# Layer 1's last turns as moves through DRAM, shared sends, and a fetch in pieces: a conv-attention and recurrence kernel in f32

## The chip, the core and the metric

The kernel runs on one core of a Trainium2 chip. The metric is the device time of one execution in microseconds, the median of several runs. A span is the part of it that the profiler sees from the first to the last instruction of the program.

## What is computed

The input x is [4, 128, 64, 64] in f32: 4 batches, 128 channels, 4096 positions. All arithmetic is f32. The reference, cut to what matters:

```python
# layer 0: attention over 4096 positions with 64 channels of q and k, gated, residual
x = x + conv_attn(group_norm(x))      # softmax(q.T k * scale), v and gate through sigmoids
# layer 1
t = x as tokens                       # [B, 4096, 128]
h = layernorm(t)
q = h @ W;  scores = q @ q.T          # symmetric: scores(n, a) is the transpose of scores(a, n)
t = t + softmax(scores) @ h
h2 = layernorm(t)
Wx = batchnorm(h2 @ Wf)               # statistics over all batches and positions
y_t = sigmoid(Wx_t + y_{t-1} @ V.T)   # recurrence over the positions
x = (t + y) as channels by positions
```

## The kernel before

The program goes through the batches one after the other: layer 0 of a batch (`layer0`), then its layer 1 (`layer1`), and after the last batch the recurrence for all of them.

**Blocks and steps.** The 4096 positions are eight blocks of 512 (`QB`, `NB`), numbered n. Layer 1 visits the query blocks in the order 6, 7, 5, 4, 3, 2, 1, 0, and for each n the key blocks a from n down to 0. Since the scores are symmetric, only a <= n is computed. One pair (n, a) takes two steps (i = 0, 1) of 256 keys each. A step computes scores on TensorE (L810), takes the exponential on ScalarE (L816), and appends the result e to a queue `fifo`; two steps later `direct` (L681) multiplies e by the values h into the sum o of block n.

**The other half of the scores.** For a < n, the transposed exponentials are needed for block a. `turn_tiles` (L651, L645) transposes 32x32 blocks on VectorE into one of two buffers dd, `send` (L661) moves these blocks to their places in one of three buffers tt by 16 DMAs from SBUF to SBUF (4 values of p times 4 of f), and four steps later `reversed_products` (L694) multiplies tt by the values of block n into `oacc` of block a. SP's queue issues the sends with f = 0, 1, 2; the four with f = 3 wait in `unsent` and are issued by ACT's queue, one entry per step, after the step's exponential.

**Blocks on the diagonal.** Where a == n > 1 (`upper`), only the upper triangle of 128x128 tiles is computed: scores of 512, 384, 256 and 128 columns. The tiles off the diagonal are turned and sent too (24 KB per DMA), and `own_products` (L671) adds them three steps later, after `direct` of that step. Blocks 0 and 1 compute the first half in full, and `quarter` (L590, L596) computes the last quarter of the scores and transposes the missing one on TensorE.

**End of a block.** When all parts of a block are in `oacc`, `finish` puts small functions into a queue `pending`; each step of layer 1 runs one of them. `tokens` transposes oacc on TensorE (L736), takes the denominators (L741), adds the residual t (L745) and takes the layer norm. `turn` transposes the normed tokens h2 on TensorE (L758) and copies them to th on ScalarE (L759); `result` writes t for the end. `inputs` multiplies th by the recurrence's weights (L767), takes the statistics and stores the result in wxs_d in DRAM, in the last batch in wxs. A placeholder `nothing` runs an item of a second queue, `ahead`, that holds the next batch's norm and projections; a step with nothing pending does the same.

**Moves.** In layer 0 a turn of 128x512 goes another way, `move`: VectorE transposes 32x32 blocks (L280), four DMAs write them to DRAM in their new order (L284), and one DMA fetches the whole (L294).

**wxs.** At the start of the last batch's layer 1 three DMAs of 2 MB fetch the recurrence's inputs of the first three batches (L947). They share a buffer with layer 0's projections, and wait until layer 0 has read these.

**Order.** The program text gives priorities; a planner with costs of its own then fixes the order of each engine's instructions, except in stretches that are marked as ordered by hand (the beginning and the end).[...]

Of the kernel before, what the change touches and what calls it, by code (L numbers as in the profile page):

```python
# [10 lines left out]
F32 = mybir.dt.float32  # L11
I32 = mybir.dt.int32
AF = mybir.ActivationFunctionType
ALU = mybir.AluOpType
# [4 lines left out]
P = 128  # L19
# [153 lines left out]
def fast(  # L173
# [17 lines left out]
    with ExitStack() as st:  # L191
# [368 lines left out]
        def layer1(b, h, qt):  # L560
# [7 lines left out]
            fifo: deque = deque()  # L568
            own_turned: deque = deque()

            unsent: deque = deque()
            turned: deque = deque()
            clock = 0
# [39 lines left out]

            def upper(n, a):

                return a == n > 1

# [45 lines left out]
            def own_products():  # L665

                _, n, t, o = own_turned.popleft()
                assert fifo and fifo[-1][0] == n
                t = t[:, : 4 * 6 * 32].rearrange("q (p s k) -> q p s k", p=4, s=6)
                for j, s in ((3, 3), (2, 1), (1, 0)):  # L670
                    nc.tensor.matmul(  # L671
                        o[:, : j * P], lhsT=h[:, NQ * n + j, :],
                        rhs=t[:, :, s : s + j, :].rearrange("q p k j -> q k p j"),
                        start=False, stop=False,
                    )
# [25 lines left out]
            def part(n, o):  # L701
# [7 lines left out]
                if parts[n] == NB - n - (b == B - 1 and n == 0):  # L709
                    finish(n)  # L710

            def finish(n):
                cs = bass.ts(n, QB)
                rinv = stat.tile([P, NQ], F32, tag="rinv", name="rinv")
                t = work.tile([P, 4, NQ, 32], F32, tag="t", name="t1", bufs=2)
                if b == B - 1 and n == 0:

                    one, two = (ep.tile([P, 2, QB], F32, tag="e", name="last") for _ in range(2))
                    h2, t1 = (one[:, r, :].rearrange("q (j c) -> q j c", j=NQ) for r in range(2))
                    th = two[:, 0, :]  # L720

                    def bank():
                        return ps_o.tile([P, QB], F32, tag="o", name="ml")
                else:
                    h2 = work.tile([P, NQ, C], F32, tag="h2", name="h2")
                    th = work.tile([P, QB], F32, tag="th", name="th")
                    t1 = work.tile([P, NQ, C], F32, tag="og", name="t1b")

                    def bank():
                        return ps_m.tile([P, QB], F32, tag="m", name="m1")  # L730
                nc.sync.dma_start(t, t_d[b, n])

                def tokens():
                    m = bank().rearrange("q (j c) -> q j c", j=NQ)
                    for j in range(NQ):
                        nc.tensor.transpose(m[:, j, :], oacc[:, n, bass.ts(j, P)], ident)  # L736
                    if b == B - 1 and n == 0:
                        take_banks()
                    at = (B + b) * NT + n * NQ
                    den = den_all[:, at : at + NQ]  # L740
                    nc.vector.tensor_reduce(den, m, AX.X, ALU.add)  # L741
                    nc.vector.tensor_scalar(den, den, 1.0 / C, None, ALU.mult)
                    nc.vector.reciprocal(rinv, den)
                    for j in range(NQ):
                        nc.vector.scalar_tensor_tensor(  # L745
                            t1[:, j, :].rearrange("q (p i) -> q p i", p=4),
                            m[:, j, :].rearrange("q (p i) -> q p i", p=4), rinv[:, j : j + 1],
                            t[:, :, j, :], ALU.mult, ALU.add,
                        )
                    layernorm(quarters(t1), quarters(h2))  # L750

                def result():
                    turn_out(t1.rearrange("q j (p i) -> q j p i", p=4), t2_d[b, :, cs])

                def turn():
                    m = bank()
                    for j in range(NQ):
                        nc.tensor.transpose(m[:, bass.ts(j, P)], h2[:, j, :], ident)  # L758
                    nc.scalar.copy(  # L759
                        th.rearrange("c (p j k) -> c j p k", j=NQ, p=4),  # L760
                        m.rearrange("c (j p k) -> c j p k", j=NQ, p=4),
                    )
                    result()

                def inputs():
                    m = bank()
                    nc.tensor.matmul(m, lhsT=wt["f"], rhs=th, start=True, stop=True)  # L767
                    nc.vector.bn_stats(bn_st[:, b * NB + n, :], m)
                    m = m.rearrange("p (g i s) -> p i g s", i=L // 2, s=2)
                    if b == B - 1 and n == 0:  # L770
                        last_inputs.append(m)
                    elif b == B - 1:
                        nc.vector.tensor_copy(wxs[:, :, b, bass.ts(n, GB), :], m)
                    else:
                        wx = work.tile([P, L // 2, GB, 2], F32, tag="wx", name="wx")
                        nc.vector.tensor_copy(wx, m)
                        nc.sync.dma_start(wxs_d[b, :, :, bass.ts(n, GB), :], wx)

                if b == B - 1 and n == 0:
                    pending.appendleft(tokens)  # L780
                    pending.extend([turn, inputs])
                elif b == B - 1 and n == 1:
                    pending.extend([tokens, nothing, turn, inputs])
                elif b == B - 1 and n < 4:
                    pending.extend([tokens, turn, inputs])
                else:
                    pending.extend([tokens, nothing, nothing, nothing, turn, inputs])


            for n in [NB - 2, NB - 1] + list(range(NB - 3, -1, -1)):  # L790
# [4 lines left out]
                for a in order(n):  # L795
# [4 lines left out]
                    for i in range(2):  # L800
                        ps = ps_s.tile([P, 2, QB], F32, tag="s", name="ps")
                        e = ep.tile([P, 2, QB], F32, tag="e", name="e")
                        if a == n < 2 and i == 1:
                            quarter(n, ps, e, before)
                        else:
                            width = 0
                            for half in range(2):
                                at = NQ * a + 2 * i + half
                                cols, scores = columns(n, a, i, half, ps)
                                nc.tensor.matmul(  # L810
                                    scores, lhsT=qt[:, bass.ts(at, P)],
                                    rhs=qt[:, n * QB + cols.start : n * QB + cols.stop],
                                    start=True, stop=True,
                                )
                                width += cols.stop - cols.start
                            nc.scalar.activation(  # L816
                                e.rearrange("p a b -> p (a b)")[:, :width],
                                ps.rearrange("p a b -> p (a b)")[:, :width], AF.Exp, bias=shift,
                            )
                            if turns(n, a) or upper(n, a):  # L820
                                turn_tiles(n, a, i, e, packed(d, n, a))
# [9 lines left out]
                            queries(NB - 1)  # L831
                        fifo.append((n, a, i, e, o))
                        clock += 1
                        if len(fifo) > LAG:
                            direct()
                            if a == order(n)[0] and i == 0:
                                direct()
                        if own_turned and own_turned[0][0] <= clock:
                            own_products()
                        if turned and turned[0][0] <= clock:  # L840
                            reversed_products()
                        if pending:
# [1 line left out]
                        elif ahead:  # L844
                            ahead.popleft()()
                    if turns(n, a) or upper(n, a):
                        send(n, a, d, t, nc.sync, range(3))
                        unsent.append(partial(send, n, a, d, t, nc.scalar, (3,)))
                    if upper(n, a):
                        own_turned.append((clock + 3, n, t, o))  # L850
                    elif turns(n, a):
# [83 lines left out]
        for b in range(B):  # L935
            xg, q, k, v = parts0
            h, qt = layer0(b, xg, q, k, v, need)
            need = lambda n, p: None
            if b < B - 1:
                parts0, norm, chunks, gates = prepare(b + 1, own_bank)  # L940
                ahead.extend(norm + sum(chunks, []) + gates)
            else:


                wxs = keep.tile([P, L // 2, B, G, 2], F32, tag="next", name="wxs")
                for i in range(B - 1):
                    nc.sync.dma_start(wxs[:, :, i, :, :], wxs_d[i])  # L947
            layer1(b, h, qt)
            while ahead:
                ahead.popleft()()  # L950
# [491 lines left out]
```

## Time and profile before

| What | Value |
|---|---|
| median of 3 runs | 3017.7 us (3017.13 to 3018.09) |
| the profiled execution, its time | 3015.99 us |
| its span | 3014.3 us |
| mean granted TensorE clock | 0.995 |
| layer 1, sends of full tiles on SP's queue | 1332 of 64 KB, 2.0 us to landing |
| layer 1, sends of full tiles on ACT's queue | 444 of 64 KB, 2.0 us to landing |
| fetches of wxs | 3 of 2048 KB, 13.8 us to landing |

How to read the profile: PE is TensorE's matrix multiplication, PEld its weight load, DVE VectorE, ACT ScalarE, POOL GpSimd, SP the engine that only issues DMAs. A "q" after an engine's name is its queue. A group line gives the line of the kernel, the engine, the operation, what it writes and reads, the shapes and the count; then the busy time in us and the mean in ns of one, and after a second bar the idle time of the engine just before these instructions, with what ended it. Lines in order of time begin with the start and the length in us. The chain gives the shares of the span on the path that ended last. An f32 matmul shows as two records, and matmuls overlap, so the distance between starts says more of the cost than the duration of one.

### The profile page before, as it was taken

To read this page: it belongs to the slowest core of one execution; us is meant where nothing else is said; L and a number is where in the kernel's file an instruction comes from. 1 tells how busy PE (TensorE), PEld (TensorE's weight loads), DVE (VectorE), ACT (ScalarE), POOL (GpSimd) and SP (SyncE) were. 2 spreads that over 40 slices of the span, in tenths; PEclk is the share of its full clock that TensorE was granted. 3 is DMA by queue.
4 is the path that set the end of the run, shared out by engine and by line. 5 is a ranking of instruction groups with operands and counts; after the bars stand their busy time and mean duration, and the time that the engine had idled before them with its cause. 6 is when DMAs were issued, how large, how long until landed. Compare 5 with 4: busy or idle time off the path is not lost.

```text
span 3014.3 us, 32549 instructions
## 1 busy us (share of the span) xinstructions
PE 2961.1 (98%) x10774; PEld 1378.9 (46%) x10774; DVE 1716.2 (57%) x3208; ACT 1016.1 (34%) x1123; POOL 223.1 (7%) x216
## 2 busy tenths in 40 slices
PE   8999999999999999999999999999999999999995
PEld 4444444444444444444444444444444444444443
DVE  6666654544666664544466666554556666344456
ACT  4444422222344432222244443222234444222224
POOL 0111100000011110000011101000001111000000
PEclk9999999999999999999999999999999999999998
DMA  1112144434122134444312114444422113544434
GB/s 42 41 54 57 50 130 105 100 95 111 31 56 57 43 90 112 102 104 106 74 46 56 42 47 127 104 106 99 106 46 56 41 48 91 147 108 104 111 94 186
DMA packets 265425, 250.62 MB, mean 83 GB/s; under 512 B 96160, under 2 KB 180640, under 8 KB 264224
## 3 DMA queue, kind: packets, MB, share of 16 engines
q1 hardware_dynamic: 239328, 216.95, 27.2%
q10 hardware_dynamic: 25920, 31.49, 4.2%
q8 instruction: 89, 1.46, 0.2%
q14 instruction: 88, 0.72, 0.1%
HBM read 65.80 MB, written 56.62 MB: 41 GB/s over the span
## 4 chain that ended last, share of the span: by engine, by line
PE 94%; DVE 2%; DMA 1%; ACT 1%; SPq 0%; issue 0%; ACTq 0%; POOL 0%; DVEq 0%
PE o L485 29%; PE o L681 15%; PE ps L243 15%; PE ps L810 14%; PE ot L694 13%; PE o L671 1%; PE m L272 1%; PE m L767 1%; PE mp L378 1%; PE mp L447 1%; DMA wxs<-wxs_d 1%; PE mp L432 1%; DVE t2s L1020 1%; DVE ps_r L991 1%; PE mq L582 1%; PE m L736 1%
## 5 line engine op out<-in xcount | busy, mean ns | idle before, releaser
L485 PE MATMUL o<-e,nxt 64*128 64x512 f32 x4096 | 966.4, 589 | 0.0
L245 ACT ACTIVATE e<-ps 128x1024 f32<-128x1024 f32 x512 | 521.6, 1025 | 687.6 <-PE ps L243 656.1
L252 DVE TENSOR_TENSOR acc<-acc,e 128x1024 f32<-128x1024 f32 x448 | 547.3, 1222 | 231.7 <-ACT e L245 216.0
L485 PEld LDWEIGHTS o<-e,nxt 64*128 64x128 f32 x4096 | 400.1, 187 | 483.0 <-issue 474.2
L816 ACT ACTIVATE e<-ps,shift 128x1024 f32<-128x1024 f32 (+2 forms) x282 | 298.7, 1060 | 729.2 <-PE ps L810 431.2
L243 PE MATMUL ps<-nxt 64*128 64x512 f32 x2048 | 533.1, 595 | 1.2 <-ACT e L245 0.6
L681 PE MATMUL o<-e,h 128*128 128x512 f32 (+3 forms) x1160 | 511.4, 567 | 0.0
L810 PE MATMUL ps<-qt 128*128 128x512 f32 (+3 forms) x1128 | 501.9, 567 | 4.0 <-ACT qt L583 2.7
L651 DVE STREAM_TRANSPOSE dd<-e 128x512 f32<-128x512 f32 x444 | 287.3, 687 | 306.2 <-ACT e L816 217.5
L694 PE MATMUL ot<-tt,h 128*128 128x512 f32 x888 | 402.2, 593 | 0.0
L681 PEld LDWEIGHTS o<-e,h 128*128 128x128 f32 x1160 | 220.2, 191 | 259.0 <-issue 248.3
L810 PEld LDWEIGHTS ps<-qt 128*128 128x128 f32 x1128 | 208.1, 190 | 230.0 <-issue 208.1
L243 PEld LDWEIGHTS ps<-nxt 64*128 64x128 f32 x2048 | 194.9, 187 | 229.6 <-issue 148.7
L694 PEld LDWEIGHTS ot<-tt,h 128*128 128x128 f32 x888 | 164.2, 190 | 186.9 <-issue 185.5
L145 POOL TENSOR_SCALAR rstd<-mv 128x4 f32<-128x4 f32 x64 | 14.6, 228 | 2349.7 <-DVE mv L309 2349.7
L703 DVE TENSOR_TENSOR oacc<-oacc,ot 128x512 f32<-128x512 f32 x87 | 59.3, 682 | 162.2 <-PE ot L694 162.2
L541 DVE SCALAR_TENSOR_TENSOR t<-yt,rinv,t 128x128 f32<-128x128 f32 x128 | 36.5, 347 | 79.6 <-DMA yt<-turn_d 79.6
L502 POOL TENSOR_SCALAR xb<-xb,bpc 128x512 f32<-128x512 f32 x32 | 63.4, 1981 | 245.1 <-DMA xb<-in_x_dram 230.5
L552 POOL TENSOR_SCALAR h<-h 128x512 f32<-128x512 f32 x32 | 72.4, 2262 | 63.8 <-DVE d L280 63.8
L146 POOL TENSOR_TENSOR rstd<-rstd,mhalf 128x4 f32<-128x4 f32 x64 | 66.4, 1038 | 5.3
L390 ACT ACTIVATE nxt<-mp,par 64x512 f32<-64x512 f32 x31 | 23.9, 772 | 114.7 <-DVE nxt L386 101.2
L312 DVE TENSOR_SCALAR h<-t,mv,rstd 128x128 f32<-128x128 f32 x128 | 35.7, 343 | 46.9 <-POOL rstd L146 46.9
(165 smaller groups left out, 1578.4 us busy)
## 6 DMA issues: line engine op xcount, KB each, us to landing
tt<-dd SPq DMA_DIRECT2D x1332, 64.0 KB, 2.0
tt<-dd ACTq DMA_DIRECT2D x444, 64.0 KB, 2.0
turn_d<-d SPq DMA_DIRECT2D x384, 64.0 KB, 1.8
nxt<-in_x_dram SPq DMA_DIRECT2D x16, 512.0 KB, 5.5
xb<-in_x_dram SPq DMA_DIRECT2D x32, 256.0 KB, 3.3
t<-turn_d SPq DMA_DIRECT2D x32, 256.0 KB, 2.7
yt<-turn_d SPq DMA_DIRECT2D x32, 256.0 KB, 2.6
t_d<-t SPq DMA_DIRECT2D x32, 256.0 KB, 2.0
```

What stands on the lines that cost most here:

```text
L146: nc.gpsimd.tensor_tensor(dst, dst, mhalf[:, :n], ALU.pow)
L243: nc.tensor.matmul(ps[:, h, :], lhsT=lhsT, rhs=rhs, start=True, stop=True)
L245: nc.scalar.activation(e, ps, AF.Exp, scale=scale)
L252: nc.vector.tensor_tensor(acc, acc, e, ALU.add)
L485: nc.tensor.matmul(o[r], lhsT=v[rs, p + h * PAIRS, :], rhs=e[rs, h, :], start=(p == 0 and h == 0), stop=(p == PAIRS - 1 and h == 1),)
L502: biased = nc.gpsimd.tensor_scalar(xb, xb, bpc, None, ALU.add)
L552: nc.gpsimd.tensor_scalar(hn, hn, 1.0, None, ALU.add)
L651: nc.vector.transpose(d.rearrange("q f b k j -> q k b f j")[:, 2 * i + half], e[:, half, :].rearrange("q (b f j) -> q b f j", b=NQ, f=NQ),)
L681: nc.tensor.matmul(o[:, cols], lhsT=h[:, NQ * a + 2 * i + half, :], rhs=es, start=(a == order(n)[0] and i == 0 and half == 0), stop=(a == ...
L694: nc.tensor.matmul(ot, lhsT=h[:, NQ * n + j, :], rhs=t.rearrange("q (p b k j) -> q b k p j", p=4, b=NQ, k=NQ)[:, j], start=(j == 0), stop= ...
L810: nc.tensor.matmul(scores, lhsT=qt[:, bass.ts(at, P)], rhs=qt[:, n * QB + cols.start : n * QB + cols.stop], start=True, stop=True,)
L816: nc.scalar.activation(e.rearrange("p a b -> p (a b)")[:, :width], ps.rearrange("p a b -> p (a b)")[:, :width], AF.Exp, bias=shift,)
```

## The change

- Blocks 4 to 7 end in `finish_moved`: oacc and h2 are turned by `move` in place of TensorE's transposes. The steps are `sums` (the move of oacc), three placeholders, `tokens` (denominators from the moved tile, residual, layer norm, the move of h2 to th, and the result), three placeholders, `inputs`.
- `upper` holds for block 1 too; `quarter` remains for block 0.
- `own_products` comes before `direct` in a step.
- For full tiles SP sends f = 0 and 1, and ACT f = 2 and 3, as two entries of `unsent`. Diagonal blocks keep 3 to 1.
- The three fetches of wxs become twelve of 512 KB, and stand in the queue `ahead`.
- `reciprocals` and `recurrence_inputs` are the old lines as functions.

```diff
             def upper(n, a):
-                return a == n > 1
+                return a == n > 0
...
+            def finish_moved(n):
+                cs = bass.ts(n, QB)
+                rinv = stat.tile([P, NQ], F32, tag="rinv", name="rinv")
+                t = work.tile([P, 4, NQ, 32], F32, tag="t", name="t1", bufs=2)
+                nc.sync.dma_start(t, t_d[b, n])
+                ot = th = None
+
+                def sums():
+                    nonlocal ot
+                    ot = work.tile([P, 4, NQ, 32], F32, tag="og", name="otk")
+                    move(oacc[:, n, :].rearrange("c (j f k) -> c j f k", j=NQ, f=4), flat(ot))
+
+                def tokens():
+                    nonlocal th
+                    reciprocals(n, ot.rearrange("q p j i -> q j p i"), AX.XY, rinv)
+                    for j in range(NQ):
+                        nc.vector.scalar_tensor_tensor(
+                            t[:, :, j, :], ot[:, :, j, :], rinv[:, j : j + 1], t[:, :, j, :],
+                            ALU.mult, ALU.add,
+                        )
+                    h2 = work.tile([P, 4, NQ, 32], F32, tag="h2", name="h2m")
+                    layernorm(tiles(t), tiles(h2))
+                    th = work.tile([P, QB], F32, tag="th", name="thm")
+                    move(h2.rearrange("q p j i -> q j p i"), th)
+                    turn_out(t.rearrange("q p j i -> q j p i"), t2_d[b, :, cs])
+
+                def inputs():
+                    recurrence_inputs(n, th, ps_m.tile([P, QB], F32, tag="m", name="mw"))
+
+                gap = [nothing] * 3
+                pending.extend([sums, *gap, tokens, *gap, inputs])
...
             def finish(n):
+                if n >= 4:
+                    return finish_moved(n)
...
-                        if a == n < 2 and i == 1:
+                        if a == n == 0 and i == 1:
                             quarter(n, ps, e, before)
...
                         clock += 1
+                        if own_turned and own_turned[0][0] <= clock:
+                            own_products()
                         if len(fifo) > LAG:
                             direct()
                             if a == order(n)[0] and i == 0:
                                 direct()
-                        if own_turned and own_turned[0][0] <= clock:
-                            own_products()
...
-                        send(n, a, d, t, nc.sync, range(3))
-                        unsent.append(partial(send, n, a, d, t, nc.scalar, (3,)))
+                        own = 3 if upper(n, a) else 2
+                        send(n, a, d, t, nc.sync, range(own))
+                        for f in range(own, NQ):
+                            unsent.append(partial(send, n, a, d, t, nc.scalar, (f,)))
...
-                for i in range(B - 1):
-                    nc.sync.dma_start(wxs[:, :, i, :, :], wxs_d[i])
+                pieces = [
+                    (wxs[:, bass.ts(r, L // 8), i, :, :], wxs_d[i, :, bass.ts(r, L // 8)])
+                    for i in range(B - 1) for r in range(4)
+                ]
+                ahead.extend(partial(nc.sync.dma_start, *piece) for piece in pieces)
```

More of the change, by code (lines that the diff above doesn't have):

```diff
@@ L667, in own_products @@
                 _, n, t, o = own_turned.popleft()
-                assert fifo and fifo[-1][0] == n
+                assert any(f[0] == n for f in fifo)
                 t = t[:, : 4 * 6 * 32].rearrange("q (p s k) -> q p s k", p=4, s=6)
@@ new lines, in reciprocals, with recurrence_inputs @@
+            def reciprocals(n, o, axes, rinv):
+                at = (B + b) * NT + n * NQ
+                den = den_all[:, at : at + NQ]
+                nc.vector.tensor_reduce(den, o, axes, ALU.add)
+                nc.vector.tensor_scalar(den, den, 1.0 / C, None, ALU.mult)
+                nc.vector.reciprocal(rinv, den)
+            def recurrence_inputs(n, th, m):
+                nc.tensor.matmul(m, lhsT=wt["f"], rhs=th, start=True, stop=True)
+                nc.vector.bn_stats(bn_st[:, b * NB + n, :], m)
+                m = m.rearrange("p (g i s) -> p i g s", i=L // 2, s=2)
+                if b == B - 1 and n == 0:
+                    last_inputs.append(m)
+                elif b == B - 1:
+                    nc.vector.tensor_copy(wxs[:, :, b, bass.ts(n, GB), :], m)
+                else:
+                    wx = work.tile([P, L // 2, GB, 2], F32, tag="wx", name="wx")
+                    nc.vector.tensor_copy(wx, m)
+                    nc.sync.dma_start(wxs_d[b, :, :, bass.ts(n, GB), :], wx)
@@ L738, in tokens @@
                         take_banks()
[L739 to L743, printed above, removed]
+                    reciprocals(n, m, AX.X, rinv)
                     for j in range(NQ):
@@ L765, in inputs @@
                 def inputs():
[L766 to L777, printed above, removed]
+                    recurrence_inputs(n, th, bank())
                 if b == B - 1 and n == 0:
```

## The prediction

> **What bounds the kernel now.** I read the page's busy times and chain first, then the groups by shape, then the order of time around layer 1, where all parts of the change lie.
>
> ```profile
> PE 2961.1 (98%) x10774; PEld 1378.9 (46%) x10774; DVE 1716.2 (57%) x3208; ACT 1016.1 (34%) x1123; POOL 223.1 (7%) x216
> ...
> PE 94%; DVE 2%; DMA 1%; ACT 1%; SPq 0%; issue 0%; ACTq 0%; POOL 0%; DVEq 0%
> ```
>
> TensorE is busy 98% of the span and 94% of the chain; no other engine exceeds 57%. In the order of time layer 1 has hardly a hole on PE, except in its first 40 us in each batch. So work taken off PE in layer 1 should shorten the span by its own length. That length is the distance between starts, not the duration of a record:
>
> ```profile
> L758 PE MATMUL m<-ident,h 128*128 128x128 f32 x124 | 19.5, 276 | 1.1 <-DVE h L312 1.1
> L736 PE MATMUL m<-ident,oacc 128*128 128x128 f32 x124 | 19.4, 279 | 0.0
> ```
>
> and in order of time (start, length, group):
>
> ```profile
> 548.23 0.60 PE L736 MATMUL m<-ident,oacc 128*128 128x128 f32 x4
> ...
> 548.67 2.74 PE L694 MATMUL ot<-tt,h 128*128 128x512 f32 x6
> ```
>
> A transpose lasts 279 ns, but four start at 548.23 and the next matmul at 548.67: 0.109 us of PE each. By the same distances a 512-column record costs 0.429 us, 384 columns 0.322, 256 columns 0.216, 128 columns 0.109; an f32 matmul has two records, a transpose one.
>
> The one large hole is the start of layer 1 in the last batch, where SP's queue, PE and the table of stretches (busy time of PE, PEld, DVE, ACT, POOL, granted clock, DMA share, GB/s) read:
>
> ```profile
> 2551.70 9.62 SPq L947 DMA_DIRECT2D wxs<-wxs_d  x3
> 2562.24 16.74 SPq L661 DMA_DIRECT2D tt<-dd  x12
> ```
>
> ```profile
> 2580.47 2.90 PE L671 MATMUL o<-tt,h 128*128 128x384 f32 x6 [2.65 <-DMA tt<-dd]
> ```
>
> ```profile
> 2579.00:2585.00 6.00, 4.53 (x9) 2.74 (x10) 2.49 (x4) 0.00 (x0) 0.00 (x0) 0.55 0.44 104
> ```
>
> The three 2 MB fetches of wxs stand ahead of the turns on SP; own_products waits for the last of these turns, and the granted clock falls to 0.55 in that window.
>
> [...]a tt<-dd issue takes 0.6 us of its queue (four on ACT in 2.44 us), and in layer 1 of one batch SP has 465 issues in 394 us, about 70% of its time.[...]
>
> **The change part by part.**
>
> 1. Turns as moves, blocks 4 to 7. Removed on PE: 4 blocks x 4 batches x 8 transposes x 0.109 = **14.0 us**. All of it lies in the middle of layer 1, without holes. ACT loses 16 copies of th at 0.586 = 9.4 us, which were covered. DVE gains 32 transposes at 0.70 = 22 us; the reduction and the four scaled additions read SBUF instead of PSUM (like rows: 347 ns against 344). Covered by DVE's 43% idle. SP gains 32 moves x 5 issues = 160. Each of them can hold SP until DVE has made the turn or the first four have landed, with later turns and loads queued behind it; the sender's reader, the th matmul, would hold PE. Layer 0 shows the price of such a chain: from L541 at 2587.29 to the landing of qt at 2599.98 it took 12.7 us, and the move of og to yt took 10.4 us in batch 0 (400.10 to 410.5). The queue gives each four steps. A step has four f32 matmuls of 512 columns and every second one four more: 5.15 us on average, so 20.6 us. Covered with 8 us to spare: I take 0; if that were wrong by 3 us at each of 16 th matmuls it would cost 48. Below zero is possible too (PSUM bank m is freed for the next batch's projections), but PE has no holes there to fill.
>
> 2. Block 1 with upper tiles only. Removed per batch: four 512-column score records 1.72, L590's four records 0.86, L596's four transposes 0.44. Added: scores 2 x (0.429+0.322+0.216+0.109) = 2.15. The products are 8 x 0.429 = 3.43 before; after, 2.15 direct and 2 x (0.322+0.216+0.109) = 1.29 in own_products, 3.45. Net 0.84 x 4 = **3.4 us**. It adds 12 issues on SP, 4 on ACT and four DVE transposes (1.4 us) per batch. Its wait for tt comes three steps after the send, behind about 15 us of scores, direct and reversed products on PE; needed are 12 x 0.6 + 2.0 = 9.2 us. I take 0, bounds 0 and 3 us per batch.
>
> 3. wxs in 12 pieces from the queue ahead. From the first L582 of layer 1 to the first L694 the last batch takes 48.2 us (2549.46 to 2597.67), batch 2 takes 30.6 (1828.15 to 1858.78). In that stretch the last batch did 26 full records more, 11.2 us of work brought forward. The rest, 17.6 - 11.2 = **6.4 us**, is the stall, and it goes. What is late next: three fetches landed in 23 us, so a piece is about 1.9 us of DMA time. Twelve spread over some twelve steps of 5.15 us add a third to a DMA load of 0.4 to 0.5. I take 1 us back; bounds 0 and 6.4 (a planner that finds SP free may issue the pieces in one go).
>
> 4. own_products before direct. In block 6 tt lands just in time: at 401.57 in batch 0, 1124.75 in batch 1, 1846.00 in batch 2, and PE reads it at 401.81, 1124.94 and 1846.24:
>
> ```profile
> 1121.90 1.88 PE L681 MATMUL o<-e,h 128*128 128x512 f32 x4
> 1124.94 1.54 PE L671 MATMUL o<-tt,h 128*128 128x384 f32 x6 [1.16 <-DMA tt<-dd]
> ```
>
> The 1.7 us of direct work that now stands ahead of the read goes behind it, so PE waits for that much longer: 1.7 to 2.0 us in three batches, 5.7 at most, 0 if the planner puts direct first. Half, **2.8 us back**. In the last batch no loads of the next input stand ahead, so no wait. Later blocks show no wait here.
>
> 5. Half of the turns by ACT. 444 issues at 0.6 leave SP and come to ACT. SP: 444 fewer, 160 + 48 more. ACT per turned block: 8 issues 4.9 us plus two exponentials 2.2 us in 10.3 us. What is queued behind is the next exponential:
>
> ```profile
> 2014.59 1.80 ACTq L661 DMA_DIRECT2D tt<-dd  x3
> 2016.49 1.11 ACT L816 ACTIVATE e<-ps,shift 128x1024 f32<-128x1024 f32 x1 [3.28 <-DMA tt<-dd]
> ```
>
> The issues began 1.4 us after an exponential, when DVE had turned it, and the next came as soon as its scores were there. PE asks for an exponential only two steps on: score, direct, score and direct, 5.1 us after the scores, minus 1.1, leaves 4.0 us of slack for four more issues (2.4 us). So 0 in the steady part. In the first eight steps, without reversed products and with a copy of qt in each second one, a step of PE is about 4.3 us and ACT needs 1.11 + 0.58 + 2.44 = 4.1: I take **2 us back** over four batches, bounds -4 (relief of SP, whose late turns hold L671) and 8.
>
> Sum: -14.0 - 3.4 - 6.4 + 1 + 2.8 + 2 = -18.0. The profiled execution took 3015.99 us (span 3014.3), which gives 2998.0; the median of the runs, 3017.7, is 1.7 above it, which gives **2999.7**.
>
> **The rivals.**
>
> A. Partial loss: the pieces are issued together after all (6.4 us lost), own_products waits in full (5.7). Gain 14.0 + 3.4 - 5.7 - 2 = about 10, time 3008. For it: SP has been seen to take fetches as soon as their buffer is free. Against it: the pieces enter the program one per step.
>
> B. Nothing left: chains of moves run late behind SP and 18 us return as waits of the th matmul, 1.1 us at each of 16: 3018. Against it are the 8 us to spare.
>
> C. Slower, by ACT: the exponential becomes what PE waits for. In a step without reversed products ACT needs 1.11 + 2.44 + 0.6 (a copy or tanh) = 4.15 us against PE's 3.43. If the next, longer step does not make up for it, each of 111 turned blocks loses 0.7 us, 78 in all; with half made up, 39 - 18 = 21 slower: 3039. It decides from 0.22 us per turned block (24 us). For it: ACT sits in order behind sends that wait for DVE, once already 7.08 us idle ahead of an exponential (421.08). Against it: 4.0 us of slack and a step of 6.9 us in every two.
>
> D. That PE's removed work was not on the path, which 94% of the chain excludes, or that wxs is not fetched in pieces, which is A.
>
> **How the numbers follow.** The forecast has 0.58 (2991 to 3006), A 0.16 (to 3012), B 0.07, C 0.19. Below 3011.7 is faster by over 0.2%, about what a measurement of this kernel can tell from no change: 0.74; within 0.2%: 0.07; above 3023.7: 0.19. The range, 2990 to 3022, takes in forecast, A and B.
>
> **What would show it.** L736 and L758 at x60 and x60 instead of x124 each, L596 at x16; no idle of over 1 us ahead of L694 in layer 1; ahead of L671 in block 6 an idle of 2 to 3 us if part 4 is right; the last batch's start like batch 2's, without a clock below 0.9 (part 3); ACT's issues of tt<-dd at x888. I am wrong if PE's idle "<-ACT e L816" grows to tens of us (C), or if PE waits for th at L767 or the line that takes its place (B).

## The result, and the profile after

The changed kernel took 3002.0 us in the median of four runs (2997.5 to 3003.5), the kernel before 3017.9 in the same series. The ratio is 0.9945, 95% interval 0.9928 to 0.9962: 16 us faster, where 18 were forecast (2999.7). The profiled execution took 3003.5 us, its span is 3001.8.

The page's busy times and chain, as shown of before:

```profile
PE 2945.3 (98%) x10654; PEld 1368.4 (46%) x10654; DVE 1741.8 (58%) x3256; ACT 1002.6 (33%) x1103; POOL 219.0 (7%) x216
...
PE 93%; DVE 2%; DMA 2%; ACT 1%; SPq 1%; issue 0%; ACTq 0%; POOL 0%
```

PE has 120 records fewer and is still 98% busy. DMA and SP's queue have grown on the chain by a point each: there to look for what was lost on the way. The groups by shape show what was removed (L792 and L810 are the old L736 and L758), and who waits for turns (L672 is own_products):

```profile
L672 PE MATMUL o<-tt,h 128*128 128x384 f32 x56 | 23.7, 507 | 4.5 <-DMA tt<-dd 4.3
...
L810 PE MATMUL m<-ident,h 128*128 128x128 f32 x60 | 10.1, 282 | 2.8 <-DVE h L312 2.8
...
L792 PE MATMUL m<-ident,oacc 128*128 128x128 f32 x60 | 9.4, 279 | 1.0 <-DVE wx L763 1.0
```

x124 became x60 twice; L597, the old L596, is at x16, and ACT issues 888 of the sends of full tiles. From the waits of PE (who waited for what: us in all, times, the longest), with the line that would have shown ACT as the new bound:

```profile
PE o L672 <- DMA tt<-dd: 4.3, 3, 3.0
PE ps_r L1052 <- DVE ps_r L1037: 3.8, 16, 0.3
PE m L810 <- DVE h L312: 2.8, 3, 1.1
PE ps L851 <- ACT qt L584: 2.7, 4, 0.7
PE ps L851 <- ACT e L857: 1.7, 4, 0.5
```

PE waits 1.7 us in all for exponentials (L857), so rival C did not come about. No th matmul of a moved block (mw, L754) waits in the whole of this view, so B did not either.

Where the time went can be read from the distance between the first query matmuls of layer 1 (L582, now L583) in successive batches. Before, they start at 383.68, 1105.77, 1828.15 and 2549.46; after, at 385.72, 1104.23, 1822.09 and 2539.78. The three full rounds are shorter by 3.6, 4.5 and 3.6 us, against 4.3 each of PE work removed. The last batch and the recurrence are shorter by 2.8 only, where the forecast's parts come to about 9. The old stall did go: from the first query matmul to the first reversed product the last batch takes 30.8 us where it took 48.2, and the granted clock is 1.00 all through. What was lost again stands later, on SP and PE:

```profile
2604.31 1.15 SPq L886 DMA_DIRECT2D wxs<-wxs_d  x2
2605.97 10.27 SPq L662 DMA_DIRECT2D tt<-dd  x8
2616.29 1.16 SPq L886 DMA_DIRECT2D wxs<-wxs_d  x2
2617.62 11.36 SPq L662 DMA_DIRECT2D tt<-dd  x12
```

```profile
2625.57 1.88 PE L851 MATMUL ps<-qt 128*128 128x512 f32 x4
2630.49 2.90 PE L672 MATMUL o<-tt,h 128*128 128x384 f32 x6 [3.04 <-DMA tt<-dd]
```

```profile
2630.00:2636.00 6.00, 5.50 (x13) 3.31 (x14) 1.30 (x2) 1.11 (x1) 0.00 (x0) 0.72 0.72 185
```

and from the waits of SP:

```profile
SPq L662 <- DMA wxs<-wxs_d: 10.5, 5, 3.5
```

The pieces of wxs (L886) leave in pairs between the turns of two blocks. The eight turns after a pair take 10.3 us to issue, not 5. An issue itself takes its usual 0.5 to 0.8 us; SP stands between the issues until a piece has landed (10.5 us in five waits in the whole batch), and a turn issued right behind the pair at 2605.97 lands after 7.3 us, where the median is 2.1. Block 7's own products wait 3.0 us; the six records after the wait take 2.90 us, in a stretch whose clock reads 0.72. The old stall stood 31 us into this layer, the new one, smaller, stands 91 us into it. In the balance of the spans, 2.0 us are missing ahead of layer 1: they were lost in the first 16 us of the program, where the ten warm-up records took 1020 ns each in the mean in this execution and 772 in that of before.

### The profile page after: what moved, and what is told of

It is laid out like the page before. It is cut to its first block, busy times and chain, and to the rows that moved or that the text cites. A ratio compares the mean times of both kernels' runs of the same rounds, so it can differ in the third digit from the quotient of the medians.

```text
span 3001.8 us, 32605 instructions
## 1 busy us (share of the span) xinstructions
PE 2945.3 (98%) x10654; PEld 1368.4 (46%) x10654; DVE 1741.8 (58%) x3256; ACT 1002.6 (33%) x1103; POOL 219.0 (7%) x216
## 4 chain that ended last, share of the span: by engine, by line
PE 93%; DVE 2%; DMA 2%; ACT 1%; SPq 1%; issue 0%; ACTq 0%; POOL 0%
PE o L485 29%; PE ps L243 15%; PE o L682 15%; PE ps L851 14%; PE ot L695 12%; PE o L672 1%; DMA tt<-dd 1%; PE m L272 1%; PE mp L378 1%; PE mp L447 1%; PE mp L432 1%; SPq L662 1%; DVE t2s L1066 1%; PE mq L583 1%; DVE ps_r L1037 1%; PE m L754 0%
## 5 line engine op out<-in xcount | busy, mean ns | idle before, releaser
L857 ACT ACTIVATE e<-ps,shift 128x1024 f32<-128x1024 f32 (+2 forms) x286 | 300.3, 1051 | 810.6 <-PE ps L851 405.9
L682 PE MATMUL o<-e,h 128*128 128x512 f32 (+3 forms) x1160 | 505.3, 562 | 0.0
L646 DVE STREAM_TRANSPOSE dd<-e 128x128 f32<-128x128 f32 (+1 forms) x112 | 35.3, 353 | 57.7 <-ACT e L857 55.1
```

The costliest lines, as they stand in the source:

```text
L682: nc.tensor.matmul(o[:, cols], lhsT=h[:, NQ * a + 2 * i + half, :], rhs=es, start=(a == order(n)[0] and i == 0 and half == 0), stop=(a == ...
L857: nc.scalar.activation(e.rearrange("p a b -> p (a b)")[:, :width], ps.rearrange("p a b -> p (a b)")[:, :width], AF.Exp, bias=shift,)
```

## The experiments

Each time is the median of at least four runs of the kernel, beside runs of the kernel before on the same chip (3016.4 us for e1 to e4, 3017.4 for e5 to e8, 3017.8 for e9 to e12). Ratios are against these. The planner orders each of these kernels but e1 anew, so an experiment changes the order of instructions too; what is said of a cause rests on the lines that wait, beside the time.

**e1, the changed kernel again.**

> The changed kernel once more, beside the three that follow. Both theories: about 3002 us, 16 us under the kernel before. What is looked for is whether the 3 us wait of the own products of block 7 in the last batch (at 2627 us) comes back in another execution. If it is made by the transfers of the wxs pieces, it comes back in about the same place, since the order of the instructions is fixed.

Measured: 2999.3 us, 0.9950 (0.9936 to 0.9963). The wait is there again, shorter:

```profile
2627.31 1.53 PE L672 MATMUL o<-tt,h 128*128 128x384 f32 x6 [1.63 <-DMA tt<-dd]
```

It comes back at the same place with the same program, and its length varies between executions.

**e2, pieces further apart.**

```diff
-                ahead.extend(partial(nc.sync.dma_start, *piece) for piece in pieces)
+                for piece in pieces:
+                    ahead.append(partial(nc.sync.dma_start, *piece))
+                    ahead.extend([lambda: None] * 2)
```

> The changed kernel with two empty places after each wxs piece in the queue ahead, so that a piece leaves in every third step and not in every step. Theory: pieces that leave in pairs hold up the turns that follow them in the DMA engines, and this is the 3.0 us wait and the slow clock after it (4.7 us). Then that wait goes and the time is about 2997 us, 4.7 under the changed kernel. Rival: the wait comes from ACT's half of the sends or from the moves; then the time stays at 3002 us and the wait stays.

Measured: 2996.1 us, 0.9937 (0.9923 to 0.9950). Block 7's own products start without a wait:

```profile
2627.83 1.46 PE L672 MATMUL o<-tt,h 128*128 128x384 f32 x6
```

SP waits less for pieces to land, too, 4.7 us against 10.3 in e1:

```profile
SPq L662 <- DMA wxs<-wxs_d: 4.7, 6, 1.4
```

So the wait came from the pieces. The gain over e1 is 3.2 us, less than the 4.7 forecast, since e1's wait was only 1.6; the intervals of the two overlap, so the trace decides here, not the times. The planner still put pieces together in twos and threes (around 2588, 2600 and 2611), but further from block 7's sends.

**e3, wxs whole.** The changed kernel with the three fetches of before.

> The changed kernel with the three 2 MB fetches of wxs as before, all else as changed. Theory: the stall of 6.4 us at the start of the last batch returns and the wait of 4.7 us at block 7 goes, so the pieces are worth only 1.7 us: 3003.7 us. Rival, the sum of the prediction: the pieces are worth 5.4 us: 3007.4 us.

Measured: 3010.0 us, 0.9981 (0.9974 to 0.9988): 10.7 us over e1, more than either theory. On PE:

```profile
2561.07 1.12 PE L583 MATMUL mq<-qt,w 128*128 128x512 f32 x2 [0.68 <-ACT qt L584]
2571.88 2.90 PE L672 MATMUL o<-tt,h 128*128 128x384 f32 x6 [9.68 <-DMA tt<-dd]
```

```profile
2561.00:2567.00 6.00, 1.12 (x2) 0.30 (x2) 0.00 (x0) 0.60 (x2) 0.00 (x0) 0.71 0.26 63
2567.00:2573.00 6.00, 1.12 (x2) 0.84 (x3) 1.14 (x2) 0.00 (x0) 0.00 (x0) 0.50 0.25 61
```

The wait at block 6's own products is 9.7 us here and was 2.65 in the kernel before. There, direct products and scores that the planner had put ahead filled most of the hole; here less stands ahead of the own products, and the clock reads 0.50 from 2567 to 2573 and 0.65 in the 6 us after (the six records take 2.90 us here and 1.46 in e2). What the pieces are worth depends on the order around them.

**e4, SP sends three quarters again.** `own = 3` for all blocks.

> The changed kernel with three quarters of all sends on SP and one on ACT, as before. SP then has 405 + 112 = 517 issues in a layer 1 of 390 us, 79% of the time at 0.6 us. Theory: the share of ACT is worth nothing by itself, sends still land in time: 3002 us, within 2. Rival: with the moves' issues on it SP is too full, turns come late to PE, and the time is 5 to 20 us longer.

Measured: 3052.8 us, 1.0125 (1.0110 to 1.0141): 53 us slower than e1. The share of ACT, which the theory put at nothing and the prediction at a cost of 2 us, carries more than the whole gain. The groups show where PE stands:

```profile
L672 PE MATMUL o<-tt,h 128*128 128x384 f32 x56 | 27.7, 580 | 33.6 <-DMA tt<-dd 32.8 <-issue 0.7
```

Own products wait 33.6 us for turns, and the mean of one has gone from 507 to 580 ns: after the longest of these waits, 5.3 us ahead of 2666.70, the clock reads 0.50 from 2667 to 2670. Exponentials are not the cause: PE waits 1.7 us for them, as in the changed kernel.

**e5, the moves alone** in the kernel before.

> The kernel before with the moves of blocks 4 to 7 alone (the new end of a block), sends, diagonal blocks and wxs as before. Theory: PE loses 128 transposes at 0.109 us on a path without holes, 14.0 us: ratio 0.9954, 3003.9 us. Rival: the moves' issues crowd SP (465 + 40 issues per layer 1, 77% of the time) and part of the gain comes back as waits for turns: 3008 to 3018 us.

Measured: 3038.8 us, 1.0073 (1.0060 to 1.0087): 21 us slower than before, past the rival's end too. Own products at the end of batch 0's layer 1:

```profile
730.17 1.54 PE L671 MATMUL o<-tt,h 128*128 128x384 f32 x6 [2.42 <-DMA tt<-dd]
```

The own products, with three steps of time against four for the others, wait first: 19.3 us in all, against 4.0 before. The th matmul of a moved block waits once, 1.6 us. That the turns leave SP late shows in how long SP stands ready ahead of a send until DVE has turned the tile, which is the room left on the queue. Before:

```profile
SPq L661 <- DVE dd L651: 111.7, 47, 5.4
```

In e5:

```profile
SPq L661 <- DVE dd L651: 19.3, 13, 3.6
```

The room has shrunk to a sixth. Its waits for the landing of earlier sends have grown meanwhile from 70.6 to 131.9 us, so SP's load is not its issues alone. That SP's lines follow one another closely for some 35 us would not tell e5 from the others: they do so before and in e10 as well.

**e6, block 1 as upper tiles alone**, with the own products first.

> The kernel before with block 1 as upper tiles alone, and the own products ahead of the direct ones, which that needs. Theory: 3.4 us less on PE, and the wait of block 6's own products moves little: 3014 us, ratio 0.9988. Rival: the own products wait 1.7 to 2.0 us longer in each batch and take it back: 3019 to 3022 us.

Measured: 3021.6 us, 1.0015 (1.0008 to 1.0021): 4 us slower. The three rounds between first query matmuls are shorter by 0.9, 0.3 and 0.1 us, so the 0.84 of PE work does go in the first of them; in the other two the own products of block 6 take most of it back (they wait 1.49 us in batch 1 and 0.58 in batch 2, where before it was 1.16 and none). The loss is in the last batch, where the stall of the whole fetch went from 2.65 to 6.03 us of wait.

**e7, half of the sends by ACT alone.**

> The kernel before with half of the full tiles' sends by ACT alone. Theory: nothing on PE changes, ACT's four more issues per turned block fit into its slack: 3017.7 us, within 2. Rival A: the exponentials come late and PE waits for them: over 3025 us. Rival B: relief of SP shortens the waits at the start of layer 1: 3012 to 3015 us.

Measured: 3022.7 us, 1.0017 (1.0010 to 1.0024): 5 us slower, and again nearly all of it in the last batch:

```profile
2585.34 2.90 PE L671 MATMUL o<-tt,h 128*128 128x384 f32 x6 [6.93 <-DMA tt<-dd]
```

The other three rounds are within 0.9 us of before, and PE waits 1.9 us for exponentials in the whole run. Rival A is refuted: ACT's slack was there. Why the hole grows with ACT's half was not separated from the planner's other order.

**e8, the pieces alone.**

> The kernel before with the wxs fetch in twelve pieces alone. Theory: the stall of 6.4 us at the start of the last batch goes, and a new one of some 4.7 us comes where pieces leave in pairs between turns: 3016 us, ratio 0.9994. Rival: the new wait belongs to the other parts, and the pieces alone give 6.4 us less: 3011.3 us, ratio 0.9979.

Measured: 3014.7 us, 0.9992 (0.9983 to 1.0000), 2.7 us under before: between the theory and the rival, nearer the theory. The profiled execution, 3012.0 us, was one of the quickest of thirteen (3012.0 to 3018.6). In it a wait of 1.6 us stands at block 7's own products (2647), so that wait comes with the pieces, without the other parts.

**e9, the moves and ACT's half together**, nothing else.

> The kernel before with the moves of blocks 4 to 7 and with half of the full tiles' sends by ACT; diagonal blocks and wxs as before. Theory after e4, e5 and e7: the moves alone lose because SP has no time left for their issues; with 112 issues a layer fewer on it the 14 us of transposes come through, and what remains is the larger stall of the whole fetch of wxs seen with ACT's half (5 us in e7): 3017.4 - 14 + 5 = 3008 us. Rival: the moves' chains themselves make PE wait, whoever sends; then it stays slower than before, 3025 us or more.

Measured: 3009.2 us, 0.9975 (0.9966 to 0.9985). Alone the two lose 21 and 5 us; together they gain 9. The rounds are 718.5, 718.6 and 718.6 us against 722.1, 722.4 and 721.3 of before: 3.6, 3.8 and 2.7 us less, against 3.5 from 32 transposes a round at 0.109 us. The moves are also all that sets e9 apart from e7. Against e7 the rounds are 3.3, 3.7 and 3.6 us shorter, and the time, each against its own kernel before, is 13.9 us less, where part 1 had 14.0.

**e10, the moves with as many issues on SP as before.**

```diff
+                        own = 2 if turns(n, a) and n_turned % 3 == 0 else 3
+                        send(n, a, d, t, nc.sync, range(own))
+                        for f in range(own, NQ):
+                            unsent.append(partial(send, n, a, d, t, nc.scalar, (f,)))
```

> As e5, the moves alone, but every third turned block has its second half sent by ACT: nine or ten blocks a layer, 36 to 40 issues, so that SP issues as many DMAs in a layer as in the kernel before (about 465). Theory: the number of issues on SP is what costs; then the loss of e5 (35 us) mostly goes and the time is 3004 to 3012 us. Rival: SP is held by the moves' waits (for DVE's transposes and for the first four landings), not by their number; then the time stays at 3030 us or more.

Measured: 3006.3 us, 0.9964 (0.9950 to 0.9978), 32 us under e5. The groups of e5, then of e10:

```profile
L671 PE MATMUL o<-tt,h 128*128 128x384 f32 x48 | 21.1, 522 | 19.3 <-DMA tt<-dd 18.5 <-issue 0.8
```

```profile
L671 PE MATMUL o<-tt,h 128*128 128x384 f32 x48 | 19.9, 496 | 4.7 <-DMA tt<-dd 4.0 <-issue 0.5
```

Most of the room on SP has come back, and SP's waits for landings of earlier sends are down from 131.9 to 73.6 us:

```profile
SPq L661 <- DVE dd L651: 79.4, 37, 5.9
```

All moves are still on SP with all their waits: ahead of the fetches (L294 <- DMA turn_d<-d) it stands 90.2 us here and 90.1 in e5. Only 40 sends a layer have left it, none of them an own product's. So what cost in e5 was the number of issues on SP, not what a move makes it wait for. Over the whole program SP issues 2382 DMAs before and in e10, 2542 in e5, 2599 in e4 and 2155 in the changed kernel.

**e11, also the diagonal blocks in halves.** e2 with `own = 2` for all blocks.

> As e2, the changed kernel with spaced pieces, and half of the diagonal blocks' sends by ACT too (eight on SP, eight on ACT). Theory: the own products wait for the last of SP's twelve sends at 0.63 us each; with eight it comes 2.5 us earlier and the waits of about 1 us at the start of each layer 1 go: 2993 us, 3 under e2. Rival: ACT's second four come one step later and are the last to land: no gain, or a loss of some us.

Measured: 2994.1 us, 0.9922 (0.9908 to 0.9935). The waits ahead of the own products at the start of each layer 1 are gone; e12, with the same sends, shows none in the whole program. Each against its own kernel before, e11 is 3.4 us under e2; the two intervals overlap, so here too it is the trace that decides.

**e12, and a step more in the last batch.**

```diff
                 elif b == B - 1 and n < 4:
-                    pending.extend([tokens, turn, inputs])
+                    pending.extend([tokens, nothing, turn, inputs])
```

> As e11, and in the last batch a step without work between the tokens and the turn of blocks 2 and 3. Theory: the transposes of h2 wait there for the layer norm by 1.1 and 0.9 us; with a step more between them these waits go: 2 us under e11. Rival: the later inputs of blocks 1 and 0 come into the final chain: 0 to 3 us over e11.

Measured: 2991.9 us (2991.2 to 2992.9; e11 had 2992.5 to 2995.5), 0.9917 (0.9904 to 0.9931): the fastest of all, 26 us under the kernel before. The waits of 0.93 and 0.78 us ahead of L810 in e11 (2841 and 2868) are gone. The chain of e12:

```profile
PE 95%; DVE 2%; ACT 1%; DMA 0%; ACTq 0%; issue 0%; SPq 0%; POOL 0%
```

DMA and SP's queue have left the chain, and PE is a point above the kernel before.

## Why the prediction was right

**The bound held.** PE, busy 98% of the span before, gave back in e9 what was taken off it: 3.4 us a round against the kernel before and 3.5 against e7, where 3.5 were forecast. The distance between starts was the right price; the 279 ns of a record would have given 36 us.

**The moves' chains were covered, but only by part 5.** Part 1 took 0 for the moves. That is right for the th matmul, which waits nowhere in the changed kernel, in e9 and in e10, and once in e5. It was wrong about what the moves do to others: e5 is 35 us above its forecast. In the profiled executions it is 33 us longer than e10, and 15 of these are longer waits of the own products; the rest is spread over smaller waits and slower records and was not followed one by one. The prediction named the later turns queued behind the moves and gave them no price. The moves' own 40 issues in a layer take about 17.5 us of SP's time (batch 0 of e5; 0.44 us each for most), on a queue whose issues filled 279 of 379 us before, 74%. Rival B had SP as the place, but the moves as what comes late and the th matmul as what waits: it was the turns that came late, and own_products that waited.

**Part 5 failed as a term of the sum and held as a part.** "2 us back" took ACT's half as a cost at the start of layer 1, with nothing in the steady part and at most 4 us of relief for SP. Against the changed kernel without it (e4) it is worth 53 us, with 444 issues fewer on SP. Taken alone, without the moves' issues on SP, it costs 5 (e7). The sum came out right because the change holds both; a sum over parts taken one by one, measured in e5 to e8, would give 3046 us. That the forecast met the time within 3 us is in part luck: two terms, the moves at 0 and ACT's half at 2, were each far off, in opposite directions.

**Part 3 was mis-sized.** The old stall, 6.4 us, was measured rightly for the kernel before. Its bound "the pieces are issued in one go" was half true: they leave in pairs, and 1.6 us (e1) to 4.5 us (the profiled execution: 3.0 of wait and 1.4 of slower records) return at block 7 instead of the 1 us taken. On the other side the whole fetch would have cost more beside the other parts: e3 is 10.7 us over e1, against the 5.4 of the sum. So the step that failed is the assumption that the stall stays at its size when the work ahead of it changes.

**Part 4 was put too high.** 2.8 us back was taken, and an idle of 2 to 3 us ahead of block 6's own products was to show it. In the profiled execution they wait 0.93 us in batch 0 and not in batches 1 and 2; before, they wait 1.16 us in batch 1 and not in the other two. In e1 there are three waits of 0.4 to 0.6. The two rounds that fall short of the 4.3 us do so by 0.8 and 0.7. The planner put the next block's scores ahead, which the prediction had not thought of, and in e11, with four sends fewer of each diagonal block on SP, the rest is gone.

**Part 2** could be seen alone in e6 alone: 0.9 us in the first round, where 0.84 was forecast, and 0.3 and 0.1 in the others, where block 6 waits longer.

Two waits at the end of the last batch were not foreseen: the transposes of h2 wait 0.93 and 0.77 us for the layer norm (L810, 2.8 us in all, against 1.1 before). e12 takes both away and is 2.2 us under e11. Waits of 0.3 to 0.8 us at the same transposes stand in e6, e7 and e8 too, where the end of a block is as before, so the new order of the small functions is not shown as their cause.

**The price of an issue.** An issue of a turn takes 0.6 us of its queue here, for a DMA that lands in 2.0, and relief of SP by 444 of them was worth 53 us in e4. The share of time that SP's issues fill would hardly have warned: in layer 1 of batch 0 it is 76% in e5 and 74% before. The wait of SP for its data, 19.3 us against 111.7, tells the two apart.

## What to carry to other kernels

Count the issues of every queue before adding moves to it, and look at how long the queue waits for its data: here that showed the room it had (111.7 us before, 19.3 in e5, 79.4 in e10). A queue whose issues filled 74% of layer 1 had no room for 40 on top of 460, though nearly every move by itself came in time; the first to suffer was the reader with the shortest deadline, own_products, which waited 19.3 us against 4.0. The two parts that share SP's queue had no separate prices here (21 and 5 us lost alone, 9 gained together): price the sum of issues on the queue, then the part that relieves it. The fetch cut into pieces helped most when the pieces were also kept apart (2996.1 us in e2 against 2999.3 in e1), and the place of the old stall should be sought again further on: it stood 31 us into the layer before, 91 us after.

## What was not expected of the hardware

Between 2382 and 2542 issues on SP, 7% more, the time rises by 32 us (e10 to e5). In the profiled executions all but 1.7 us of it comes after the first layer 1 has begun.

The same program differs between executions in two places. Layer 1 began at 385.72 us in the profiled execution of the changed kernel and at 384.17 in e1: two warm-up records near 11 us took 2.06 us in the one and 1.10 in the other. The last batch and the recurrence took 3.2 us more in the first, where block 7 waits 3.0 us and not 1.6. Together these are nearly all of the 5.0 us between the two executions.
